# The conditioner's units in pairs, four of the seven products of a unit each split into seven smaller ones

## The chip, the cores and the metric

The kernel runs on one core of a Trainium2 chip, in fp32. The metric is the device time of a whole run, in microseconds (us). The engines are TensorE (PE; matrix products), VectorE (DVE) and GpSimd (POOL; both element-wise), ScalarE (ACT; copies and functions) and SyncE (SP, which here issues DMAs). PE reads weights and tokens from SBUF and writes to PSUM, which has eight banks of 128 partitions x 512 columns.

## The reference

x holds 1024 tokens of 512 features. Two blocks are added to it in turn; the change touches the first stage of the first block, the conditioner.

```python
# the conditioner: 512 -> 1376 -> 512, with an adapter of rank 16 chosen for each batch
gate = lora_add(einsum('bnh,fh->bnf', x, W_gate), x, A_gate, B_gate)
up   = lora_add(einsum('bnh,fh->bnf', x, W_up),   x, A_up,   B_up)
act  = silu(gate) * up
down = lora_add(einsum('bnf,hf->bnh', act, W_down), act, A_down, B_down)
# the first feed-forward layer: 512 -> 1792 -> 512, weights w * (su @ sv) of rank 4
d = silu(linear(down, gate_w, ...)) * linear(down, up_w, ...)
x = x + linear(d, down_w, ...)
# then a second block of the same kind, on the new x: one product with adapters, and int4 weights with scales
```

## The kernel before

**Stages.** Features lie on the partitions, tokens on the columns. The order of the work is: the conditioner's gate and up ("c"), its down projection (down_c), the first feed-forward layer's gate and up ("f") and down, then the second block (layers "l" and "q"). Gate and up are worked through in units of 128 hidden features: 11 units in c (1376 padded to 1408), 14 in f.

**Seven products.** gate_up (L543) computes one unit. It sees the unit's two weight blocks (gate, up) by two halves of the features as a 2x2 matrix, and the tokens likewise as two halves of the features by two halves of the tokens (TB = 512 columns). Instead of eight block products it makes seven, after Strassen and Winograd: products 1 to 7, each of two matmuls of 128x128 weights by 128x512 tokens into one bank (product, L352). Four weight forms (s1 to s4, differences of weight blocks) are made on DVE or POOL by gate_up_forms (L389) and weight_forms (L297), and four token forms T1 to T4 once for all units. DVE adds the banks up into act; ACT takes the silu; POOL multiplies (L606, L611). The adapters come in as eight small matmuls of 32 rows a unit (gate_up_adapters, L966).

**Pairs in layer f.** Units 0 and 1 of f go through gate_up. The others go in six pairs through two_units (L1122). There products 2, 7, 4 and 3 of the two units are split once more: the two units of the pair and two halves of the features give the second level its 2x2 weights, two halves of 256 columns its tokens, so that each of the four becomes seven small matmuls of 128x256 (`small`, L1143), 28 in a pair, and the other three products of each unit stay full. `pair` (L1153) computes two of the four at a time: banks z1 (za1, zb1) and z5 (za5, zb5) take the small products that several outputs share, ACT copies z1 into the result tiles r2, r7 (or r4, r3) and DVE adds z5 at `fifth`. The second-level weight forms are made by POOL in forms_of (L1098), the second-level token forms by DVE once. A pair ends with `finish`, which multiplies the first half of act, and last_silu, which is called in the next pair.

**The order in c.** The loop (from L990) takes units 0 to 10 in turn. prepare_c (L525) loads a unit's weights three units ahead, makes its forms one unit ahead, and at units 8 to 10 loads f's first weights, scales them (scale_f: small products "pw" of scale factors on PE, five a call, then three multiplications on DVE) and makes their first forms. In the same loop stand the splitting and joining of the scale factors (scale_piece: a memset, DMAs by SP, a copy on ACT, a subtraction on POOL, and at the join L474 and L476 on DVE), the gathering of adapter rows for down (POOL, L222) and the loads of the down weights (L383, from unit 3 on, into wd_all).

**What sets the order.** Each engine runs its instructions in the order in which the program lists them (in_order), and waits there for what the others have not yet done. All matmuls but those of layer q go through the helper mm, and carry its line, L88, in the profile. PSUM banks are handed out in turn from a pool of eight: a product's first matmul waits until the last reader of its bank's former content is through.

Of the kernel before, what the change touches and what calls it, by code (L numbers as in the profile page):

```python
# [7 lines left out]
F32 = mybir.dt.float32  # L8
# [5 lines left out]
P = 128  # L14
NB = 8
# [17 lines left out]
AHEAD = 3  # L33
# [22 lines left out]
def kernel(  # L56
# [468 lines left out]
    def prepare_c(f: int):  # L525

        if f + AHEAD < NF0:
            load_c(f + AHEAD)
        if f + AHEAD - 1 < NF0:
            finish_c(f + AHEAD - 1)  # L530
        if f == NF0 - 3:
            load_f(0)
            load_f_down(0)
        if f >= NF0 - 2:
            scale_f(0, f - NF0 + 2)()
        if f == NF0 - 1:
            load_f(1)
            gate_up_forms("f", (0, 1), nc.gpsimd)
# [4 lines left out]
    def gate_up(  # L543
# [69 lines left out]
        for tb in range(NTB):  # L613
            acts[f, tb] = act[tb]
        return finish
# [259 lines left out]
    with ExitStack() as c_layer:  # L875
# [90 lines left out]
        def gate_up_adapters(f: int):  # L966
            def add(banks, fresh, go_on):
                for q2 in range(2):
                    for tb in range(NTB):
                        for s in range(2):  # L970
                            rows = rows4(tb, s)
                            mm(
                                banks[s][tb][:, bass.ts(q2, TG)],
                                b_rows4[rows, q2, bass.ts(f, P)], t0[0][rows, bass.ts(q2, TG)],
                                start=(s, tb) in fresh, stop=(s, tb) in fresh or q2 == 1,
                                skip_group_check=(s, tb) in go_on,
                            )

            return add

        def unit_temp(f: int):
            return lambda what: temps.tile([P, TB], F32, tag=what, name=f"{what}_c{f}", bufs=2)


        first_unit = None
# [6 lines left out]
        for f in range(NF0):  # L992
            prepare_c(f)
            if 2 <= f <= 6:
                join_piece = split_piece()
            if 1 <= f <= 5:
                split_piece = scale_piece(temps, f - 1)
            if f >= 3:
                for of in range(f - 3, f - 2 if f < NF0 - 1 else NF0):
                    load_c_down(of)  # L1000
            if f == 2:
# [3 lines left out]
            if 3 <= f < 7:  # L1005
                down_adapters_a.gather(range(2 * f - 6, 2 * f - 4))
            if f == 8:
                down_adapters_a.arrange(nc.scalar.copy, slice(0, NB))
            finishing = gate_up(
                [act_c[:, f, tb] for tb in range(NTB)], unit_temp(f), "c", f, b_x, gate_up_adapters(f), f == 0, f == NF0 - 1,  # L1010
                (first_low_rank, first_unit) if f == 1 else (),
            )
            if f:
                finishing()
            else:
                first_unit = finishing
            if 2 <= f <= 6:
                join_piece()
# [8 lines left out]
        def down_low_rank():  # L1027
# [5 lines left out]
            )  # L1033

# [17 lines left out]
        with ExitStack() as top:  # L1052
# [4 lines left out]
                {1: down_low_rank, 6: three_forms}, down_adapters,  # L1057
# [6 lines left out]
    with ExitStack() as top:  # L1064
# [5 lines left out]
        def second_tokens(i: int, src: str):  # L1070

            b1, b2 = b_h[src]
            left, right = (bass.ts(q, TB // 2) for q in range(2))
            t = {"3": b1[:, right]}
            for w in ("1", "2", "4"):
                t[w] = temps.tile([P, TB // 2], F32, tag=f"T{w}_{i}", name=f"T{w}_{i}")
            for w, x1, x2 in (
                ("1", b1[:, right], b1[:, left]), ("2", b2[:, right], t["1"]),
                ("4", b2[:, left], t["2"]),
            ):  # L1080
                in_order(nc.vector.tensor_tensor(t[w], x1, x2, ALU.subtract))
            tokens2[i] = {
                1: b1[:, left], 2: b2[:, left], 3: b2[:, right], 4: t["4"],
                5: t["1"], 6: t["2"], 7: t["3"],
            }
# [6 lines left out]
        def scaling(n: int):  # L1092

            return (
                lambda: scale_f(n, 0)(), lambda: scale_f(n, 1)(), lambda: forms_of(n)
            )

        def forms_of(n: int):  # L1098
            a = ready["f", "second", n] = {}
            raw = ready["f", "raw", n]  # L1100

            def second_forms(products, of):
                forms = temps.tile(
                    [P, len(products), 4, P], F32, tag=f"s{products[0]}", name=f"s{products[0]}_{n}"
                ).rearrange("p i w f -> p w i f")
                blocks = [
                    of[:, u].rearrange("p (i c) f -> p c i f", c=2)[:, c]
                    for u in range(2) for c in range(2)
                ]
                weight_forms(nc.gpsimd, *blocks, *(forms[:, w] for w in range(3)), True, s3_to=forms[:, 3])  # L1110
                for j, i in enumerate(products):
                    w11, w12, _, w22 = (w[:, j] for w in blocks)
                    s1, s2, s4, s3 = (forms[:, w, j] for w in range(4))
                    a[i] = {1: w11, 2: w12, 7: s3, 4: w22, 5: s1, 6: s2, 3: s4}

            gate_up_forms(
                "f", (2 * n, 2 * n + 1), nc.gpsimd, True, lambda: second_forms((2, 7), raw[:, :, 2:6])
            )
            second_forms((4,), raw[:, :, 6:8])
            second_forms((3,), ready["f", "s", n][:, :, 4:6])  # L1120

        def two_units(n: int, tail):  # L1122

            fs = (2 * n, 2 * n + 1)
            a, a2 = [ready["f", f] for f in fs], ready["f", "second", n]
            act = [[act_all[:, f, tb] for tb in range(NTB)] for f in fs]
            for f, both in zip(fs, act):
                for tb in range(NTB):  # L1130
                    acts[f, tb] = both[tb]
            two = range(2)

            def temp(what: str, tag: str, bufs: int = 1):
                return temps.tile([P, 2, TB], F32, tag=tag, name=f"{what}_f{n}", bufs=bufs)

            def banks(i):
                return [bank(f"p{i}_f{n}_{u}") for u in two]

            def full(ps, u: int, i: int, src: str):  # L1140
                product(ps, a[u][i], b_h[src], True, True)

            def small(ps, at: int, i: int, j: int, start: bool):  # L1143

                mm(
                    ps[:, bass.ts(at, TB // 2)], a2[i][j], tokens2[i][j], start=start, stop=True,
                    skip_group_check=not start,
                )

            def add(to, x1, x2):  # L1150
                in_order(nc.vector.tensor_tensor(to, x1, x2, ALU.add))

            def pair(z: str, r, order, at):  # L1153

                z1, z5 = (bank(f"z{z}{i}_f{n}") for i in (1, 5))

                def both(ps, j: int, start: bool):  # L1160
                    for m, i in enumerate(order):
                        small(ps, m, i, j, start and m == 0)

                def copied(blocks: slice):
                    size = blocks.stop - blocks.start
                    for m in two:
                        src = z1[:, bass.ts(m, TB // 2)]
                        if size > 1:
                            src = src.unsqueeze(1).to_broadcast([P, size, TB // 2])
                            in_order(nc.scalar.copy(r[m][:, blocks], src))  # L1170
                        else:
                            in_order(nc.scalar.copy(r[m][:, blocks.start], src))

                both(z1, 1, True)
                copied(slice(0, 1))
                both(z5, 5, True)
                at(0)
                both(z1, 6, False)
                copied(slice(1, 2))
                at(1)  # L1180
                both(z1, 7, False)
                copied(slice(2, 4))
                at(2)

                def fifth():
                    for m in two:
                        to = r[m].rearrange("p (i j) t -> p i j t", j=2)[:, :, 1]
                        src = z5[:, bass.ts(m, TB // 2)]
                        add(to, src.unsqueeze(1).to_broadcast([P, 2, TB // 2]), to)

                return fifth

            def r_tile(what: str):
                return temps.tile([P, 4, TB // 2], F32, tag=what, name=f"{what}_f{n}")

            def all_of(r):
# [573 lines left out]
```

## Time and profile before

| | us |
|---|---|
| median of 3 runs (lowest, highest) | 673.28 (672.62, 673.37) |
| the profiled execution | 673.58 |
| its span, first to last instruction | 671.8 |
| c unit 2 | 37.51 to 50.80 |
| c units 3 and 4 | 50.80 to 77.38 |
| c units 9 and 10 | 130.76 to 157.57 |
| down_c | 157.57 to 229.41 |
| one pair of f | 284.02 to 307.67 |

The profile gives for each group of instructions its line, the engine, the operation, the tiles out<-in, shape and count; a timeline gives each stretch of like instructions with its start. "PE p_c" is a conditioner product, "p_f", "za_f", "zb_f" those of layer f, "pw" a scale product. A matmul in fp32 leaves two records. The idle time ahead of a group is given with what ended it.

### The profile page before, as it was taken

The numbers are of one execution on the slowest core, as the hardware profiler recorded it, in microseconds if no ns is written. First come the engines' busy times: TensorE is split into PE (matmuls) and PEld (weight loads), VectorE is DVE, ScalarE is ACT, GpSimd is POOL, SyncE is SP. The second block draws the span as 40 slices with busy tenths as digits, with TensorE's granted clock in tenths as the row PEclk, the third lists the DMA queues.
The fourth block names the chain that finished last, engine by engine and source line by source line (L and its number), as shares of the span: only waits on it lengthen the run. The fifth ranks groups of instructions, "written<-read, shape, count | busy, mean of one in ns | idle before, by whom it ended". The sixth has DMA issues, their size and how long they took to land.

```text
span 671.8 us, 7259 instructions
## 1 busy us (share of the span) xinstructions
PE 661.1 (98%) x2534; PEld 408.3 (61%) x2534; DVE 513.3 (76%) x675; ACT 194.4 (29%) x294; POOL 414.5 (62%) x362
## 2 busy tenths in 40 slices
PE   8999999999999999999999999999999999999995
PEld 3444444444667645666666664785536777788874
DVE  5545544446988996877878689999857888899997
ACT  1122111211111112334323421110115555655563
POOL 5356774432771045668766930898602989898996
PEclk9999999999999999999999999999999999999998
DMA  6501124255002002202200050000931220000003
GB/s 236 201 0 54 64 72 160 93 126 20 1 0 79 32 0 95 94 1 94 95 1 0 1 173 30 1 4 13 344 126 31 55 71 17 17 0 1 0 1 125
DMA packets 39715, 42.48 MB, mean 63 GB/s; under 512 B 24624, under 2 KB 25680, under 8 KB 39552
## 3 DMA queue, kind: packets, MB, share of 16 engines
q1 hardware_dynamic: 33152, 25.71, 12.8%
q0 software_dynamic: 5376, 14.49, 6.9%
q10 hardware_dynamic: 1152, 1.84, 0.8%
q8 instruction: 20, 0.33, 0.2%
q14 instruction: 15, 0.12, 0.1%
HBM read 39.93 MB, written 2.10 MB: 63 GB/s over the span
## 4 chain that ended last, share of the span: by engine, by line
PE 84%; issue 7%; POOL 6%; DVE 1%; DMA 1%; ACT 1%; SPq 0%; POOLq 0%; DVEq 0%; ACTq 0%
PE p_c L88 21%; PE p_f L88 13%; PE gu_q L1485 12%; PE d_f L88 9%; PE d_q L1485 5%; PE d_c L88 5%; PE l L88 4%; PE z_f L88 3%; PE zb_f L88 3%; PE za_f L88 3%; PE z_c L88 2%; POOL sum L1500 1%; PE bank L1485 1%; DMA raw_c<-in_c_gu_dram 1%; POOL act_lo L1500 1%
## 5 line engine op out<-in xcount | busy, mean ns | idle before, releaser
L1494 DVE SCALAR_TENSOR_TENSOR sum<-gu_q,sg,sum 128x1024 f32<-128x1024 f32 x65 | 83.1, 1282 | 15.4 <-ACT sum L1491 10.3
L1485 PE MATMUL gu_q<-h_hi,wgu_q 128*128 128x512 f32 x208 | 82.0, 394 | 0.6 <-DVE l_v L1429 0.4
L1485 PE MATMUL gu_q<-h_lo,wgu_q 128*128 128x512 f32 x208 | 81.1, 390 | 0.0
L88 PE MATMUL p_f<-x,s_f 128*128 128x512 f32 x112 | 52.2, 597 | 0.0
L1500 POOL TENSOR_TENSOR sum<-sum,sum 128x1024 f32<-128x1024 f32 (+1 forms) x14 | 32.6, 2330 | 27.9 <-DVE sum L1494 27.9
L1491 ACT ACTIVATE sum<-gu_q,sg 128x1024 f32<-128x1024 f32 x39 | 43.3, 1112 | 21.6 <-PE gu_q L1485 21.6
L605 DVE TENSOR_TENSOR act_c<-p_c,v_c 128x512 f32<-128x512 f32 x11 | 7.6, 690 | 52.3 <-PE p_c L88 52.3
L1485 PEld LDWEIGHTS gu_q<-h_hi,wgu_q 128*128 128x128 f32 x208 | 39.0, 188 | 12.7 <-DVE x L1494 2.6
L1485 PEld LDWEIGHTS gu_q<-h_lo,wgu_q 128*128 128x128 f32 x208 | 39.1, 188 | 7.9
L88 PE MATMUL p_c<-x,raw_c 128*128 128x512 f32 x88 | 43.1, 610 | 0.5 <-DMA x<-in_xT_dram 0.5
L1500 POOL TENSOR_TENSOR act_lo<-sum,act_hi 128x1024 fp32r<-128x1024 f32 (+1 forms) x15 | 33.9, 2259 | 13.3 <-ACT act_hi L1552 13.3
L1494 DVE SCALAR_TENSOR_TENSOR x<-d_q,sd,x 128x1024 f32<-128x1024 f32 x33 | 42.0, 1274 | 0.0
L88 PE MATMUL p_c<-T_x,raw_c 128*128 128x512 f32 x88 | 41.6, 594 | 0.0
L88 PE MATMUL p_c<-T_x,s_c 128*128 128x512 f32 x88 | 41.2, 592 | 0.0
L88 PE MATMUL p_f<-h,raw_f 128*128 128x512 f32 (+1 forms) x96 | 40.2, 541 | 0.1
L606 POOL TENSOR_TENSOR act_c<-act_c,p_c 128x512 f32<-128x512 f32 x10 | 12.8, 1279 | 41.9 <-DVE act_c L605 33.1
L1500 POOL TENSOR_TENSOR sum<-sum,sil_q 128x1024 f32<-128x1024 f32 (+1 forms) x15 | 33.9, 2261 | 1.6 <-ACT sil_q L1543 1.4
L1485 PE MATMUL d_q<-act_hi,wd_q 128*128 128x512 f32 x88 | 34.8, 396 | 0.0
L1485 PE MATMUL d_q<-act_lo,wd_q 128*128 128x512 f32 x88 | 34.3, 390 | 0.0
L88 PEld LDWEIGHTS p_f<-x,s_f 128*128 128x128 f32 x112 | 20.9, 190 | 19.5 <-issue 16.7
L88 PEld LDWEIGHTS p_c<-T_x,raw_c 128*128 128x128 f32 x88 | 16.6, 190 | 21.4 <-issue 20.5
L88 PEld LDWEIGHTS p_c<-T_x,s_c 128*128 128x128 f32 x88 | 16.7, 190 | 21.0 <-issue 20.3
(349 smaller groups left out, 1519.5 us busy)
## 6 DMA issues: line engine op xcount, KB each, us to landing
raw_f<-in_f_gu_dram SPq DMA_DIRECT2D x14, 512.0 KB
wgu_q<-in_q_gu_dram POOLq DMA_DIRECT2D x14, 512.0 KB
raw_c<-in_c_gu_dram SPq DMA_DIRECT2D x10, 512.0 KB
wd<-in_f_down_dram SPq DMA_DIRECT2D x14, 256.0 KB
wd_q<-in_q_down_dram POOLq DMA_DIRECT2D x14, 256.0 KB
x<-in_xT_dram SPq DMA_DIRECT2D x11, 256.0 KB
wd<-in_c_down_dram SPq DMA_DIRECT2D x11, 256.0 KB
out_dram<-x SPq DMA_DIRECT2D x6, 256.0 KB
```

Of the source, the lines that this page charges most:

```text
L88: in_order(nc_mm(*args, **kwargs))
L605: add(act[0], x4, v, ALU.add)
L606: mul(act[0], act[0], p1, ALU.mult)
L1485: nc.tensor.matmul(ps, w, part[:, at], start=(n == 0), stop=(n == len(src) - 1))
L1491: in_order(nc.scalar.activation(to, ps, AF.Identity, scale=scale))
L1494: nc.vector.scalar_tensor_tensor(to, ps, scale, plus, op0=ALU.mult, op1=ALU.add)
L1500: in_order(nc.gpsimd.tensor_tensor(to, a, b, op))
```

## The change

c's units 2 to 9 are computed in four pairs by the same two_units, which is now a function for both layers. Units 0 and 1 are computed as before, and unit 10 stays single and comes last.

- two_units takes the layer, its tokens and tiles, three callbacks (`amid`), and for c the adapters. With adapters, eight small matmuls for each unit of the pair come at the end of the pair, into two of its product banks and two new ones.
- The second-level tokens (16 subtractions of 256 columns, DVE) are made once, after unit 1, in wd_all's first eight slots, the second-level weight forms in the slots 8 to 11. So the down weights (c's eleven, and f's first two) can't come until the last pair is through: their loads, and those of f's second pair of units, move into unit 10.
- POOL makes all weight forms for a pair in the pair before; those of products 4 and 3 (`rest`, eight operations) at the start of the pair itself.
- Splitting and joining a scale piece happens once in a pair, the last join after unit 10. The gathers for down's adapters come by three, three and two in the first three pairs. Both calls of scale_f for f's first pair come inside unit 10, between its products; their DVE multiplications queue behind the last pair's finishing adds. f's first forms go from unit 10 to a hook inside down_c.
- The result tiles r4 and r3 lie where the up adapters were, r2 in the act of unit 10 or a tile, in turn; p1, u and r7 have one tile each.

```diff
+        tiles = {
+            "r4": up_adapters.raw.rearrange("p b c -> p (b c)"),
+            "r3": up_adapters.a.rearrange("p c b -> p (c b)"),
+        }
+        for what in ("p1", "u", "r7", "r2"):
+            tiles[what] = temps.tile([P, T], F32, tag=what, name=f"{what}_c")
...
+        def second_tokens():
+            for n, (i, src) in enumerate(((2, "21"), (7, "T3"), (4, "T4"), (3, "22"))):
+                places = wd_all[:, 2 * n : 2 * n + 2].rearrange("p i (h t) -> p (i h) t", h=2)
+                tokens2[i] = tokens_of_blocks(b_x[src], *(places[:, j] for j in range(4)))
+
+        def forms_to(products):
+            first = {2: 8, 4: 10, 3: 11}[products[0]]
+            return wd_all[:, first : first + len(products)].rearrange("p i (w f) -> p i w f", f=P)
...
-        for f in range(NF0):
-            prepare_c(f)
-            if 2 <= f <= 6:
-                join_piece = split_piece()
-            if 1 <= f <= 5:
-                split_piece = scale_piece(temps, f - 1)
-            if f >= 3:
-                for of in range(f - 3, f - 2 if f < NF0 - 1 else NF0):
-                    load_c_down(of)
...
+        finishing = unit_c(1, (first_low_rank, first_unit))
+        finishing()
+        second_tokens()
+        rest_of = None
+        for n in range(1, NF0 // 2):
+            for f in (2 * n + 4, 2 * n + 5):
+                if f < NF0:
+                    load_c(f)
+            if n == NF0 // 2 - 1:
+                load_f(0)
+            join_piece = pieces[-1]()
+            if n == 1:
                 a_down_rows, b_down_rows, a1_rows, b1_rows = late_rows()
                 gather_rows(b0_down, b_table, b_down_rows)
                 down_adapters_a = Adapters(l0, temps, "0d", a_table, a_down_rows, NF0)
+            if n < 4:
+                down_adapters_a.gather(range(3 * n - 3, min(3 * n, NB)))
+            else:
                 down_adapters_a.arrange(nc.scalar.copy, slice(0, NB))
+
+            def next_piece():
                 join_piece()
+                pieces.append(scale_piece(temps, n))
+
+            def next_forms():
+                if n + 1 < NF0 // 2:
+                    rest_of_forms.append(forms_of_pair("c", n + 1, forms_to))
+                else:
+                    finish_c(NF0 - 1)
+
+            rest_of = two_units(
+                "c", n, b_x, tokens2, act_c, tiles.get, lambda: spare if n % 2 else tiles["r2"],
+                (lambda r: lambda: r and r(nc.gpsimd.tensor_tensor))(rest_of),
+                (rest_of_forms[-1], next_piece, next_forms), gate_up_adapters,
+            )
+        join_piece = pieces[-1]()
+        load_f_down(0)
+        for f in range(NF0):
+            load_c_down(f)
+        load_f(1)
+
+        def rest_and_scale():
+            silus.append(rest_of(nc.gpsimd.tensor_tensor))
+            scale_f(0, 0)()
+
+        def silus_and_scale():
+            for u in range(2):
+                silus[0](u)
+            scale_f(0, 1)()
+
+        silus = []
+        unit_c(NF0 - 1, (rest_and_scale, silus_and_scale))()
+        join_piece()
...
+        if adapters is None:
...
+        else:
+            for u in two:
+                x1, x8 = (bank(f"p{i}_{layer}{n}_{u}") for i in (9, 8))
+                adapters(fs[u])(
+                    [[x1, b5[u]], [b4[u], x8]], {(0, 0), (1, 1)} | ({(1, 0, 1)} if u else set()),
+                    {(0, 1), (1, 0)},
+                )
+                if u == 0:
+                    fifth43()
+                add(c11[u], x1, c11[u])
+                in_order(nc.scalar.activation(c11[u], c11[u], AF.Silu))
+                add(act[u][0], b4[u], v[u])
+                add(u_[:, u], b5[u], u_[:, u])
+                add(act[u][1], x8, act[u][1])
```

## The prediction

> **What bounds the kernel now.** I read, in this order: busy time by engine, the chain of work that ended last, a table by stage, and the timeline of TensorE (PE) and of the engines beside it. First the busy times and the engines' shares of the chain:
>
> ```profile
> PE 661.1 (98%) x2534; PEld 408.3 (61%) x2534; DVE 513.3 (76%) x675; ACT 194.4 (29%) x294; POOL 414.5 (62%) x362
> PE 84%; issue 7%; POOL 6%; DVE 1%; DMA 1%; ACT 1%; SPq 0%; POOLq 0%; DVEq 0%; ACTq 0%
> ```
>
> PE is busy 98% of the span, so a product less counts, and so does every wait put in front of PE. The stages that matter (columns: stretch, sum, then each engine's busy time with its instructions, granted clock, DMA share, GB/s):
>
> ```profile
> 37.51:50.80 13.29, 13.29 (x49) 5.96 (x45) 6.07 (x14) 2.22 (x4) 6.52 (x7) 1.00 0.00 0
> 50.80:77.38 26.58, 26.58 (x93) 11.92 (x89) 12.10 (x16) 4.74 (x8) 17.39 (x19) 1.00 0.19 60
> 130.76:157.57 26.81, 26.81 (x97) 12.31 (x94) 11.41 (x18) 3.49 (x6) 10.02 (x8) 1.00 0.55 81
> 157.57:229.41 71.84, 71.84 (x337) 47.02 (x333) 66.54 (x86) 11.56 (x24) 30.05 (x28) 1.00 0.12 23
> 284.02:307.67 23.65, 23.65 (x94) 15.63 (x91) 18.85 (x28) 8.30 (x19) 17.89 (x21) 1.00 0.20 68
> ```
>
> The rows are: unit 2 of the conditioner; its units 3 and 4; its units 9 and 10; its down projection; one pair of units of the second layer, which already has the new form. PE has no gap in any, at the full granted clock, while VectorE (DVE) and GpSimd (POOL) have slack in the first three. A pair in the new form has 28 DVE instructions where two units have 16: the slack is what the change spends.
>
> **The products.** The prices come from PE's timeline, start to start:
>
> ```profile
> 52.62 1.88 PE L88 MATMUL p_c<-T_x,s_c 128*128 128x512 f32 x4
> 54.33 1.88 PE L88 MATMUL p_c<-T_x,raw_c 128*128 128x512 f32 x4
> ...
> 284.99 1.03 PE L88 MATMUL za_f<-T,s 128*128 128x256 f32 x4
> 285.85 0.59 PE L88 MATMUL p_f<-h,raw_f 128*128 128x256 f32 x2
> 286.28 1.03 PE L88 MATMUL za_f<-T,s 128*128 128x256 f32 x4
> ```
>
> A full product (two matmuls, four records) takes 54.33 - 52.62 = 1.71 us, 1.716 over a unit; a small one (one matmul 256 wide, two records) 286.28 - 285.85 = 0.43 us, 0.4316 over the pair. A unit's eight adapter matmuls take 1.08 us and 0.1 on each side, since 7 x 1.716 = 12.01 and the unit takes 13.29.
>
> [...] The row decides: 0.4316 is half of one full-width matmul's 0.858 within 1%, in fp32, with weight loads busy for 15.63 of the pair's 23.65 us.
>
> A new pair is then 6 full products (10.30), 28 small (12.08) and two adapter groups (2.36): **24.74 us against 26.58**, -1.84 each, -7.36 for the four pairs (2,3), (4,5), (6,7), (8,9). Unit 10 keeps its form (13.29), but both groups of scale products pw now stand between its products. Where they stood at a unit's end they cost 0.22 each; inside pairs of the second layer, 0.63 (0.43 and 0.1 on each side). So +0.82. PE itself gains **6.55 us**; what follows is given back as waits.
>
> **What DVE and POOL do to one another.** This decides the waits:
>
> ```profile
> 105.89 0.34 DVE L474 TENSOR_SCALAR scale_parts<-scale_parts,keep 128x256 fp32r<-128x256 f32 x1
> 106.27 3.36 DVE L476 SCALAR_TENSOR_TENSOR scale_parts<-scale_raw,keep,scale_parts 128x256 fp32r<-128x256 f32 x1
> ...
> 106.80 1.27 POOL L606 TENSOR_TENSOR act_c<-act_c,p_c 128x512 f32<-128x512 f32 x1
> 108.02 1.27 POOL L611 TENSOR_TENSOR act_c<-act_c,u_c 128x512 f32<-128x512 f32 x1
> ```
>
> A DVE operation with two SBUF inputs, 0.34 us by its width, ended 0.34 us after the second POOL multiplication. DVE adds that read PSUM keep about 0.6 us each beside POOL. [...]
>
> **A: the tokens of the second level, start of the first pair.** Sixteen subtractions of 256 columns (0.34 us, 5.4 in sum) are issued in a block when unit 1's last add is done at 39.44, ahead of the small index operations and of the pair's first add. POOL runs unit 1's multiplications to 41.0 and then the subtraction of a scale piece (1.28). The second product of za5 needs the fifth subtraction. With no collision that is 39.44 + 5 x 0.36 = 41.2; behind the two multiplications and the subtraction 43.5. PE wants it at 42.3. Cost 0 to 1.2, with 2 if the block's tail also holds up the first adds; I take **1.0**.
>
> **B: the rest of the pair's weight forms.** Eight POOL operations of 128 columns stand behind the gathers for b_down and three of ga_0d (1.3 us apart), which wait for DVE's index rows at about 48.0. The gathers end at 52.8, and the first form that zb5's second product needs at 56.6, when PE wants it. Cost 0 to 1.7; **0.3**.
>
> **C: the pair's edges.** At a pair's end DVE's fifth adds free the bank of the next p1 with about 0.1 us to spare. In the next pair ACT has the silus of c12, which wait for a 1024-wide DVE add that ends 6.9 us in (7.7 to 8.9 in the last pair, where POOL's multiplications collide with it), ahead of the copies of za1 that za7 waits for: 0.1 each in the second and third, 0.85 in the last. The joining of a scale piece (1.64 where its width alone needs 0.6) stands ahead of DVE adds that free banks for b5: 0.4. Together **1.6** (0.4 to 4).
>
> **D: unit 10.** pw_0_1_2 takes the bank of pw_0_0_0, which is free when DVE has scaled raw_f with it. On DVE this stands behind the add of product 5 (7.5 us into the unit) and three finishing adds of the last pair, two of 512 and one of 1024 columns. With 0.6, 0.6, 1.22 and 0.6 it ends 10.5 us in; PE wants the bank at 9.45. Cost 1.05. In the second layer's pairs the same kind of adds take 2.29 us for two and 1.47 for the wide one beside POOL: 11.9, cost 2.4. Each waiting as the 3.36 above did: 13.2, cost 3.7. POOL is idle when the first begins, so the low half of these: **1.8**. Behind the waiting PE stand unit 10's last two products and adapters, and all of down.
>
> **Moves that I cost at nothing.** Eleven down weights of the conditioner, two of the second layer, and its second pair of gate and up weights go to unit 10's time, since their places hold scratch. They are 3.4 MB ahead of what is needed first; at the 340 to 420 GB/s that the trace shows in its busiest microseconds that is about 9 us, and they land 7 to 9 us into a unit of over 14.5. SP issues them in 15 x 0.45 = 6.8 us; behind them sd (11.38 us of SP's time) comes some 10 us later and is for a layer far behind. The second layer's first forms (5.1 us of POOL) go into down: POOL is busy there for 30 of 71.84 us, and its forms due next have some 20 us. The last scale piece (1.2 us of DVE) goes ahead of down's first forms; later DVE has an idle 3.3 us there that takes it. The loads of c units come in pairs, 0.45 us each of SP, all ahead of their use by a pair. If the cover of these fails it is the weights that are late, the third rival.
>
> **Sum.** -6.55 + 1.0 + 0.3 + 1.6 + 1.8 = **-1.85 us** on the profiled execution (673.58, span 671.8 and 1.8 around it), so 671.7; it lies 0.3 above the median of the runs, so 671.4 against 673.28. I say **671.5**. With all low ends the costs are 1.5 and the gain 5.0; with all high ones 11.4 and a loss of 4.9.
>
> **Rivals.** [...] *The other side, POOL becomes the bound* (0.30). In the second pair POOL has a subtraction 1.28, three gathers 3.9, the rest 5.35, silu multiplications 2.5, a memset 0.53, the next forms 8.3 and two multiplications 2.5: 24.4 against PE's 24.74; the first has about 23, the third 23.1. In the conditioner's down, with DVE as busy as it will be now, POOL's 256-wide operations take 0.86 to 1.17 instead of 0.73. With 0.2 us more on some 20 operations the pairs need 26.5, 27.5 and 26.5, and PE waits for the rest forms: about 5.3 us in sum. -6.55 + 5.3 + 1.0 + 1.6 + 1.8 = +3.2, **676.5**. It decides from about 24.8 us of POOL work in a pair; against it, the second layer's pairs keep pace with 17.9. *The weights are late* (0.04): at under 170 GB/s, 3.4 MB take 20 us and down starts some 5 us late: **677**. That small products aren't there at all can be left out: each pair's instructions hold 28 of them.
>
> **How the numbers follow.** The likeliest case, the gain mostly given back, has 0.38 (669.7 to 673.3 alone). Within 0.2% (1.35 us), about what a measurement of this kernel can tell from no change, lies a third of it and a little of the others. Faster 0.48, same 0.19, slower 0.33. The range for 8 in 10 takes in the first rival's and most of the second's: 667.8 to 677.0.
>
> **What would show it.** In the profile after: pairs of about 25 to 26 us between starts of p1, PE gaps before za5 in the first pair and before pw_0_1_2 in unit 10, and down with 71.8 us as before. A gap before zb5 with POOL as releaser in each pair would show the second rival; one released by a DMA at down's start the third. Wrong at its root would be a small product over 0.45 us here.

## The result, and the profile after

The changed kernel takes 677.0 us (676.75 to 678.9, 5 runs) against 673.28 (672.62 to 673.37): 1.0066 times as long, 95% interval 1.005 to 1.0083. I had forecast 671.5 and a range up to 677.0 with a gain as the likeliest. The profiled execution took 678.9 us, span 677.1; two of the five runs lie near it and three near 676.8. One stretch of 3.41 us more or less at half the clock (below) would make 1.7 us, about that difference; this is an estimate, since only the one run has a trace.

The page of the kernel after, busy times and chain:

```profile
PE 661.2 (98%) x2630; PEld 429.8 (63%) x2630; DVE 550.6 (81%) x735; ACT 212.2 (31%) x342; POOL 446.1 (66%) x398
PE 76%; DVE 8%; issue 8%; POOL 5%; ACT 1%; DMA 1%; SPq 0%; DVEq 0%; POOLq 0%; ACTq 0%
```

PE's busy time is the same as before, 661.2 us to 661.1, although some 6.5 us of products were taken away; DVE now has 8% of the chain where it had 1%. The stages (stretch, sum, busy time of PE, PE's weight loads, DVE, ACT and POOL, then the granted clock, DMA share, GB/s); the rows are the first, second and last pair, unit 10 up to the end of its scale products, and the rest of unit 10:

```profile
37.51:65.00 27.49, 25.74 (x116) 16.75 (x112) 21.97 (x44) 7.95 (x18) 18.96 (x23) 1.00 0.15 46
65.00:90.33 25.33, 25.27 (x113) 16.83 (x112) 19.47 (x27) 8.68 (x20) 22.02 (x25) 1.00 0.15 53
...
115.61:141.85 26.24, 25.72 (x114) 16.76 (x113) 18.76 (x27) 9.69 (x21) 16.46 (x20) 1.00 0.16 57
141.85:154.49 12.64, 10.52 (x32) 4.41 (x31) 10.52 (x16) 2.71 (x6) 4.83 (x4) 0.97 1.02 317
154.49:162.13 7.64, 7.64 (x25) 3.24 (x24) 2.21 (x4) 0.00 (x0) 4.35 (x5) 0.61 1.61 7
```

No pair reaches 24.74 us, the best take 25.3. In unit 10 the rest, two products and the adapters, takes 7.64 us for what takes 4.7 at full clock (151.55 to 156.26 in the first experiment): the granted clock is 0.61 there. Down starts at 162.13 instead of 157.57, so 4.56 of the 5.3 us that the span has grown are lost by then.

PE's timeline in unit 10:

```profile
149.35 1.98 PE L87 MATMUL p_c<-T_x,raw_c 128*128 128x512 f32 x4
151.26 0.38 PE L87 MATMUL pw<-scale_parts 16*128 16x256 f32 x2
153.77 0.79 PE L87 MATMUL pw<-scale_parts 16*128 16x512 f32 x3 [2.12 <-DVE raw_f L516]
154.49 3.78 PE L87 MATMUL p_c<-x,raw_c 128*128 128x512 f32 x4
158.06 3.07 PE L87 MATMUL p_c<-x,s_c 128*128 128x512 f32 x4
```

The third pw of the second group waits 2.12 us for its bank, and then a full product that takes 1.72 us elsewhere takes 158.06 - 154.49 = 3.57. DVE and POOL ahead of it:

```profile
149.63 1.28 DVE L679 TENSOR_TENSOR act_c<-act_c,ga 128x512 f32<-128x512 f32 x2
150.83 2.29 DVE L679 TENSOR_TENSOR ga<-ga,u_c 128x1024 f32<-128x1024 f32 x1
153.04 1.27 DVE L516 TENSOR_TENSOR raw_f<-raw_f,pw 128x512 f32<-128x512 f32 x2
...
150.39 3.86 POOL L825 TENSOR_TENSOR act_c<-act_c,r_c 128x512 f32<-128x512 f32 x2 [4.84 <-DVE act_c L679]
```

The two narrow adds run unhindered; the wide one takes 2.29 us beside POOL's first multiplication (1.22 without it, in the second experiment), and POOL's two take 3.86 for 2.5. The clock, in steps of one us (columns as above):

```profile
152.00:153.00 1.00, 0.00 (x0) 0.00 (x0) 1.00 (x1) 0.00 (x0) 1.00 (x2) 1.00 1.05 422
153.00:154.00 1.00, 0.23 (x3) 0.24 (x3) 1.00 (x3) 0.79 (x2) 1.00 (x1) 0.81 1.23 154
154.00:155.00 1.00, 1.00 (x4) 0.56 (x5) 1.00 (x3) 0.36 (x1) 1.00 (x2) 0.50 1.54 11
...
160.00:161.00 1.00, 1.00 (x2) 0.11 (x1) 0.00 (x0) 0.00 (x0) 0.00 (x0) 0.78 1.32 5
161.00:162.00 1.00, 1.00 (x17) 0.72 (x16) 0.00 (x0) 0.00 (x0) 0.00 (x0) 1.00 0.77 6
```

It falls to 0.50 at the end of the wait and stays there for 6.8 us (153.61 to 160.44), which costs an estimated 3.4, half of it. And the 25.3 us of an undisturbed pair come from its end; PE and DVE there, in the first pair:

```profile
62.31 2.76 PE L87 MATMUL p_c<-t_gu,b_rows 32*128 32x256 f32 x32
65.00 3.70 PE L87 MATMUL p_c<-x,raw_c 128*128 128x512 f32 x8
...
62.61 1.29 DVE L679 TENSOR_TENSOR ga<-zb_c,ga 128x512 f32<-128x512 f32 x2 [4.41 <-ACT ga L698]
```

The sixteen adapter matmuls take 65.00 - 62.31 = 2.69 us where eight take 1.08 elsewhere. In steps of 0.05 us PE is idle at 63.9, just when DVE's two adds of zb5 end (62.61 + 1.29).

### The profile page after: what moved, and what is told of

The parts are those of the page before. It is cut to its first block, busy times and chain, and to the rows that moved or that the text cites. A ratio compares the mean times of both kernels' runs of the same rounds, so it can differ in the third digit from the quotient of the medians.

```text
span 677.1 us, 7591 instructions
## 1 busy us (share of the span) xinstructions
PE 661.2 (98%) x2630; PEld 429.8 (63%) x2630; DVE 550.6 (81%) x735; ACT 212.2 (31%) x342; POOL 446.1 (66%) x398
## 4 chain that ended last, share of the span: by engine, by line
PE 76%; DVE 8%; issue 8%; POOL 5%; ACT 1%; DMA 1%; SPq 0%; DVEq 0%; POOLq 0%; ACTq 0%
PE p_f L87 13%; PE p_c L87 12%; PE gu_q L1577 12%; PE d_f L87 9%; PE d_q L1577 5%; PE d_c L87 5%; PE l L87 4%; PE z_f L87 3%; PE zb_f L87 3%; PE za_f L87 3%; PE zb_c L87 2%; DVE x L1586 2%; PE z_c L87 2%; DVE sum L1586 2%; DVE ga L679 1%
## 5 line engine op out<-in xcount | busy, mean ns | idle before, releaser
L308 POOL TENSOR_TENSOR wd<-wd 128x256 f32<-128x256 f32 (+1 forms) x6 | 8.5, 1424 | 38.5 <-DVE ds_f L868 23.4
L301 POOL TENSOR_TENSOR s_f<-raw_f 128x512 f32<-128x512 f32 x7 | 10.3, 1476 | 33.0 <-DVE raw_f L516 33.0
L87 PE MATMUL p_c<-x,raw_c 128*128 128x512 f32 (+1 forms) x64 | 31.6, 624 | 0.2 <-DMA x<-in_xT_dram 0.2
L87 PE MATMUL d_c<-act_c,wd 128*128 128x512 f32 (+1 forms) x72 | 28.2, 526 | 0.0
L87 PEld LDWEIGHTS p_f<-h,raw_f 128*128 128x128 f32 x96 | 18.1, 190 | 15.5 <-issue 13.8
```

The lines of the kernel that those rows point to most:

```text
L87: in_order(nc_mm(*args, **kwargs))
L301: in_order(engine.tensor_tensor(s1, a21, a22, ALU.add))
L308: made = engine.tensor_tensor(to, x1, x2, ALU.subtract)
```

## The experiments

Where a kernel has one run, spans are compared; a span lies about 1.8 us under its run's time. The kernel after has a span of 677.1, the one before 671.8. Unit 2, with which the first pair begins, started between 36.81 and 38.36 us in all these traces, ahead of every edit, so a difference of spans of about 1 us says little by itself; smaller effects are read from the lines.

**The scale products' multiplications ahead of the adds.**

```diff
         def rest_and_scale():
-            silus.append(rest_of(nc.gpsimd.tensor_tensor))
             scale_f(0, 0)()
+            silus.append(rest_of(nc.gpsimd.tensor_tensor))
```

> In unit 10 the three multiplications with the first scale products are put ahead of the last pair's finishing adds on DVE; nothing else. Theory: the 2.1 us wait of PE before the third pw product falls away, and with it the stretch of 6.8 us at half the granted clock that follows it (153.8 to 160.6), which costs about 3.2 us: unit 10 takes about 15 us instead of 20.28, the run 671.7. Rival 1: the clock falls because of what else happens in unit 10 (3.4 MB of DMA at a share above 1.0), not because of the wait: the wait goes, the low clock stays, 674.9. Rival 2: the wait only moves to the next product or to down's first form, which now stand behind the delayed adds: 676 to 677.

Measured: 672.72 us (672.38 to 673.36), 0.9993 times the kernel before (0.9984 to 1.0002), span 671.3. PE's timeline:

```profile
151.12 0.50 PE L87 MATMUL pw<-scale_parts 16*128 16x256 f32 x5
151.55 1.98 PE L87 MATMUL p_c<-x,raw_c 128*128 128x512 f32 x4
153.37 1.88 PE L87 MATMUL p_c<-x,s_c 128*128 128x512 f32 x4
...
156.26 8.85 PE L87 MATMUL d_c<-act_c,wd 128*128 128x512 f32 x20
```

The wait is gone and the clock is 1.00, with the DMA as before: unit 10 takes 14.56 us (141.70 to 156.26) instead of 20.28, where I had worked out 14.55 without a wait. Two lines in another order are worth 5.8 us between the profiled spans (4.3 between the medians): about 3.4 for the clock, worked out as half of 6.8, and the other 2.3 for the wait of 2.12 and the restart behind it. The DMA alone doesn't bring the clock down (rival 1): its share is 1.35 from 149.00 to 156.26 here, and 1.32 from 149 to 157 in the kernel after. Nothing moved on (rival 2).

**The wide add first.**

```diff
+                if n == NF0 // 2 - 1:
+                    add(all_of(r3), all_of(r3), u_.rearrange("p u t -> p (u t)"))
                 for u in two:
                     add(act[u][0], act[u][0], c21[:, bass.ts(u, TB)])
             for u in two:
                 in_order(mul(act[u][0], act[u][0], c11[u], ALU.mult))
-            add(all_of(r3), all_of(r3), u_.rearrange("p u t -> p (u t)"))
```

> In the last pair's finish the 1024-wide add goes ahead of the two 512-wide ones, so that POOL's multiplications start only behind it. Theory: the wide add took 2.29 us for 1.22 because it stood behind POOL; without that, PE's wait is about 1.1 us instead of 2.1. The first pair's wait of about 1.1 left the clock at 1.00; if the clock falls by the length of a wait, it stays up here too, and the run takes about 672.8. Rival: the length isn't what counts, any wait in this stage brings the clock down: about 675.9. Second rival: the collision with POOL isn't the cause of the 2.29: wait 2.1 as before, 677.

Measured: 674.19 us, span 672.4, PE's wait before that pw 1.05 us, the product behind it at full pace (154.42 - 152.60 = 1.82 us), the mean granted clock 0.997 as in runs of the kernel before (0.997 to 0.999). The wide add:

```profile
149.10 1.22 DVE L679 TENSOR_TENSOR ga<-ga,u_c 128x1024 f32<-128x1024 f32 x1
```

So the collision with POOL made half of the wait, and a wait of half the length leaves the clock up: the step from 1.05 to 2.12 us of waiting costs 4.7 us of span.

**What brings the clock down: waits put into the kernel before.**

```diff
+                def stall(f=f, dummy=act_c[:, NF0 - 1, 0]):    # between products 5 and 4 of unit f
+                    for _ in range(STALLS[f]):
+                        in_order(nc.vector.memset(dummy, 0.0))
+                    mm(bank(f"stall_{f}"), ready["c", f][4][0], dummy, start=True, stop=True)
```

> The kernel before, with a wait of PE put into units 3 to 8 of the conditioner ahead of product 4: PE there takes one more matmul (0.86 us) that needs a chain of 1, 2, 3, 4, 6 and 8 memsets of 512 columns on DVE, behind DVE's add of product 5. Waits of about 0.7 us plus 0.3 to 0.5 for each memset, so about 1.1 to 3.1, or to 4.9. No DMA to speak of in most of these units. Theory: up to some length of wait, between 1.1 and 2.1 us, the granted clock stays at 1.00 and the unit is longer by the wait and 0.86; above it the clock is 0.50 for 3 to 7 us and the unit longer by another 1.7 to 3.4. Rival: the low clock needs unit 10's DMA, and no unit here shows it.

> The kernel before with one memset ahead of the extra matmul in each of units 3 to 8: six equal gaps of 2.07 us, 16.46 us apart. In the run with growing stalls the clock fell only at the end of stretches of 3.41 us in which PE had done nothing, 20.48 us (six such stretches) apart, and gaps of 2.07, 2.73 and 3.39 that lay across the edge of two such stretches left it at 1.00. In the changed kernel a gap of 2.1 us brought it down for two such stretches. Theory: the clock is judged by the share of idle time in stretches of 3.41 us that run on by themselves; at 0.46 busy it stays, at about 0.35 it falls. The gaps here move by 0.18 of a stretch from one to the next, so two or three of six lie within one stretch (busy share 0.39) and bring the clock down, the others don't. Rival: only a whole idle stretch counts, none falls, and what fell in unit 10 has a further cause, the matmuls of 16 rows beside the gap or the DMA.

> The kernel before with two memsets ahead of the extra matmul in each of units 3 to 8: six gaps of 2.07 us, 16.46 us or 4.82 stretches of 3.41 us apart, so that each lies 0.18 of a stretch further. The run with one memset had gaps of 1.42 only, and none brought the clock down. Theory: the idle share of a stretch decides; two or three of the six gaps lie within one stretch (idle share 0.61) and bring the clock to 0.50 for 3.41 us or twice that, 1.7 or 3.4 us each: span between 693 and 700. Rival: 0.61 isn't enough either, clock 1.00 throughout, span 671.8 + 6 x 2.95 = 689.5; then the gap in unit 10 must have had help from what stood beside it.

Growing waits (span 703.2): the gaps were 1.42, 2.07, 2.73, 3.39, 4.71 and 6.02 us. Up to 3.39 the clock stayed at 1.00; behind 4.71 and 6.02 it was at 0.50 for 3.4 and 6.8 us. It fell at 129.07 and 149.55, 20.48 us or six stretches of 3.41 apart, and both gaps held a whole such stretch. By that a gap of 2.1 us could not have brought it down. Six equal gaps: they came out at 1.42 us, not 2.07 as I wrote in the expectation, because one memset was too few; none brought the clock down (span 687.9), which tells nothing on 2.07. With two memsets (span 695.3):

```profile
76.75 1.10 PE L89 MATMUL stall<-act_c,raw_c 128*128 128x512 f32 x2 [2.08 <-DVE act_c L1015]
93.20 1.56 PE L89 MATMUL stall<-act_c,raw_c 128*128 128x512 f32 x2 [2.07 <-DVE act_c L1015]
111.36 1.10 PE L89 MATMUL stall<-act_c,raw_c 128*128 128x512 f32 x2 [2.08 <-DVE act_c L1015]
127.82 2.04 PE L89 MATMUL stall<-act_c,raw_c 128*128 128x512 f32 x2 [2.08 <-DVE act_c L1015]
145.98 1.10 PE L89 MATMUL stall<-act_c,raw_c 128*128 128x512 f32 x2 [2.07 <-DVE act_c L1015]
```

Two of six equal gaps brought it down, at 93.69 and 127.83, ten stretches of 3.41 us apart: the matmul behind them takes 1.56 and 2.04 us instead of 1.10. Laid over these stretches, the two gaps lie wholly inside one (2.07 of 3.41 us idle, 0.61). The gap before 76.75 has 1.96 us in one stretch (0.57) and left the clock up, like the others, which are cut further in. So these runs fit a clock that is judged stretch by stretch: it fell where PE idled for 0.61 of one and was left at 1.00 where it idled for 0.57. The beat doesn't come with the program: this kernel and the one with growing waits differ only in how many memsets stand in a wait, and counted from the start of the span the clock fell at 127.83 us in the one and at 129.07 in the other, 1.24 us or 0.36 of a stretch apart. The growing waits agree: no stretch that left the clock up was idle for more than 1.89 us (0.55). The matmul behind a gap reads zeros, but that doesn't make it count as idle: the stretch from 108.59 to 112.00 in that run had 1.55 us of idle time and 0.93 of such a matmul, 0.73 together, and the clock stayed.

**Matmuls of few rows beside the wait.** In unit 10, 1.97 us of gap (0.58) lay in the stretch from 150.20 to 153.61, hardly more than what left the clock up here, but pw matmuls of 16 rows stood beside it.

```diff
-                    mm(bank(f"stall_{f}"), ready["c", f][4][0], dummy, start=True, stop=True)
+                    mm(to, w[:16], b_x["11"][0][:16], start=True, stop=True)    # ahead of the gap
+                    mm(to, w[:16], dummy[:16], start=True, stop=True)           # behind it
```

> The same with three memsets and with two matmuls of 16 rows (0.86 us each) in place of the one of 128 rows, one ahead of the gap and one behind, as the scale products stand beside the gap of unit 10: gaps of about 1.87 us between 0.86 us of 16-row work on each side. Theory if 16 rows count as little activity: low activity lasts 3.6 us, over half of a stretch lies in it for any position, and the clock falls in most of the six units. Rival: a matmul counts whatever its rows, the gaps of 1.87 do no more than those of 2.07: clock 1.00, span 671.8 + 6 x 3.6 = 693.

Measured: gaps of 1.59 us, not 1.87, shorter than any above that counted, and the clock fell in all six units, once for 3.4 and five times for 6.8 us (span 713.4, mean granted clock 0.971). In the second of the units:

```profile
76.11 1.12 PE L89 MATMUL stall<-x,raw_c 16*128 16x512 f32 x2
78.82 2.07 PE L89 MATMUL stall<-act_c,raw_c 16*128 16x512 f32 x2 [1.59 <-DVE act_c L1015]
80.81 3.78 PE L89 MATMUL p_c<-T_x,raw_c 128*128 128x512 f32 x4
```

Had only idle time counted, none could have: 1.59 us is 0.47 of a stretch, and 0.57 was too little. So 16-row matmuls count for less than others. How much less can be bounded: the stretch that ended at 78.54 had 1.32 us of idle time and 1.12 of 16-row work, so to pass the 1.96 that left the clock up, over half of that work must count as idle, if one share decides in both runs. The six are not six independent cases: the units came 20.44 to 20.48 us apart, six stretches, so the last five lay almost alike on the beat. By this the scale products beside the wait of unit 10, 0.38 us in its stretch, add to what counts as idle there. Whether its gap of 0.58, between the 0.57 that stayed and the 0.61 that fell, would have done it without them isn't shown.

The traces also tell one stretch from two. The clock stayed low for a second stretch where the first low one again held idle time and 16-row work of 0.94 us or more (0.15 and 0.79 in the kernel after, from 153.61 to 157.03), and came back after one where these were at most 0.17 us. Between the two nothing was measured.

**The tokens in two parts.**

```diff
-        second_tokens()
+        second_tokens(((0, 2, "21"), (1, 7, "T3")))     # the steps of the two products in turn
...
                 a_down_rows, b_down_rows, a1_rows, b1_rows = late_rows()
+                second_tokens(((2, 4, "T4"), (3, 3, "22")))
```

> The second-level tokens of products 2 and 7 are made step by step in turn, so that za5's second product needs the second subtraction, not the fifth; the tokens of products 4 and 3 come after the index rows for the gathers, which so start about 3 us earlier. Theory: the waits of 1.24 us before za5 and 0.78 before zb5 in the first pair fall away, the pair takes 25.4 us instead of 27.49: 675.0. Rival: the eight subtractions left ahead of the first add still hold back the freeing of banks, and at most one of the two waits goes: 676.

Measured: span 675.2 (676.98 us), the first pair 25.27 us (37.78 to 63.05) and both waits gone. -1.9 us of span, as the theory had it; the wait of unit 10 and its low clock were the same as in the kernel after.

**The adapters in another order.**

```diff
+                places = [(q2, tb, s) for q2 in range(2) for tb in range(NTB) for s in range(2)]
+                if (1, 0, 1) in fresh:                   # the second unit of a pair
+                    places.sort(key=lambda place: place[1:] == (1, 1))
```

> On top of the kernel with the scale products' multiplications first (profiled span 671.3, 672.7): in each pair the second unit's two adapter matmuls into the bank of x8 go last of its eight. That bank is the one of zb5, which DVE's two fifth adds free 1.5 us after the first unit's adapters begin. The adapters of a pair took 2.69 us instead of 2 x 1.08. Theory: the missing 0.53 us is PE waiting for that bank; moved back by six matmuls the wait shrinks to about 0.1, so -0.4 in each of four pairs: span 669.7. Rival: sixteen matmuls of 32 rows in a row are simply slower, or the wait is of the whole group: no change, 671.3.

Measured: span 672.4. PE's idle moment disappeared, but the sixteen matmuls took 2.69 us as before, so this run said nothing for the bank. It became plain beside the others: the next product started 1.11 us behind the end of DVE's adds of zb5 here too (64.75 and 65.86), because the last two matmuls, which alone need the bank, now ran one behind the other. The 1.0 us that the span is longer than in the kernel with the scale products first is there when the first pair starts (38.36 against 37.35 us), ahead of the edit.

> The three edits together: scale products' multiplications first, tokens in two parts, second x8 last. Theory: the waits that they take away are apart from one another, so the gains add: 672.7 - 2.0 - 1.6 = 669.1, 0.6% under the kernel before. Rival: with PE earlier, DVE and POOL are late at the next place, and half of the 3.6 comes back: 671.

Measured: 670.85 us (670.57 to 671.1), 0.9964 (0.995 to 0.9977): 1.9 below the first edit alone, all from the tokens. Neither the theory's 669.1 nor the rival's reason.

**The last pair.**

```diff
-            else:
-                down_adapters_a.arrange(nc.scalar.copy, slice(0, NB))
...
             def next_piece():
+                if n == 4:
+                    down_adapters_a.arrange(nc.scalar.copy, slice(0, NB))
```

> The three edits, the wide add ahead of the two narrower ones at every pair's end, and ACT's copy of the gathered rows for down (1.36 us) moved from the start of the last pair to its middle. Theory: the two waits of za in the last pair (that pair took 26.24 us, its neighbour 25.28) come from that copy, which stands ahead of the copies of p1 and za1, and from the wide add behind POOL's multiplications, so -0.9 against the three edits: 668.2. Rival: only one of the two counts, 668.7.

Measured: 669.65 us (669.49 to 670.07), 0.9946 (0.9933 to 0.996). -1.2; no wait of za in the last pair is left. Both causes went in one run; their shares are read from the kernel after, where PE lost 0.34 us before the za behind ACT's copy of the gathered rows, and 0.43 before the one behind the silu that waits for the wide add.

**The adds of zb5 in two steps.**

```diff
             copied(slice(1, 2))
+            if split:                                    # z == "b", with adapters
+                for m in two:
+                    add(r[m][:, 1], z5[:, bass.ts(m, TB // 2)], r[m][:, 1])
             at(1)
...
-                    add(to, src.unsqueeze(1).to_broadcast([P, 2, TB // 2]), to)
+                    add(r[m][:, 3], src, r[m][:, 3])
```

> The kernel with scale first, tokens in two parts, wide add first and ACT's copy moved, without the reordering of the adapters. New: the adds of zb5 at a pair's end are cut in two, those onto the second blocks (two of 256 columns) made earlier, right behind ACT's copies of these blocks, when DVE idles for over 2 us; at the end only two of 256 columns are left (0.7 us in place of 1.2). In every kernel so far, the reordered one too, the next product started 1.10 to 1.12 us behind the end of these adds. Theory: they set when the second unit's adapters get their bank; they end 0.45 us earlier, so each pair is 0.45 shorter: 669.6 - 1.8 = 667.8. Rival: matmuls of 32 rows set the 2.69 us themselves: 669.6 as without it, or more, for four more DVE instructions a pair.

Measured: 668.2 us (668.16 to 668.93), 0.9925 times the kernel before (0.9911 to 0.9938). PE, and DVE beside it, at the first pair's end:

```profile
59.85 2.39 PE L87 MATMUL p_c<-t_gu,b_rows 32*128 32x256 f32 x32
...
60.15 0.91 DVE L679 TENSOR_TENSOR ga<-zb_c,ga 128x256 f32<-128x256 f32 x2 [1.62 <-ACT ga L698]
```

The adds end at 61.06 and the next product starts at 62.17, again 1.11 later; the sixteen matmuls take 2.32 us, so 0.37 of the 0.53 us is gone in each pair. DVE's adds set the end of a pair, and still do, by the 0.16 us that 2.32 is over 2 x 1.08. No other wait of PE shows in the conditioner's pairs; they take 24.9 to 25.1 us.

**More work for POOL.**

```diff
         def rest():
+            if layer == "c" and n in (2, 3):
+                in_order(nc.gpsimd.memset(dummy[:, 1], 0.0))
+                for _ in range(4):
+                    in_order(nc.gpsimd.tensor_tensor(dummy[:, 0], dummy[:, 1], dummy[:, 1], ALU.subtract))
```

> On top of the kernel with the scale products' multiplications first (span 671.3): POOL gets a memset and four subtractions of 512 columns that nothing uses (0.5 + 4 x 1.28 = 5.6 us), ahead of the eight rest forms of the second and third pair. There POOL is busy about 22 of 25.3 us. Theory: what decides isn't the sum but when a form is due: the first rest form that zb5 needs is ready about 3.8 us early in the second pair, so PE waits about 1.8 us in each of the two pairs, and the forms of the next pair, which are 1.4 us early, follow late: 675 in span. Rival (the second one of the prediction): POOL has no room, all 5.6 us come through in both pairs: 682. Other rival: it is hidden altogether, 671.3.

Measured: span 679.0, +7.7, of which 0.4 is there at the start of the first pair. The second pair took 29.47 us and the third 28.36, so of 5.6 us 4.1 and 3.1 came through. What PE waited for (0.6 of the first row belongs to the first pair):

```profile
PE zb_c L87 <- POOL wd L301: 3.5, 4, 1.6
PE zb_c L87 <- ACT ga L705: 3.1, 2, 1.6
```

The forms were late by 2.9 us in the two pairs, where I had worked out 3.6; as much again came by way of ACT, whose copies of zb1 go into the tile that POOL's last multiplications still read. So for work ahead of the rest forms POOL had 1.5 us to spare in the second pair and 2.5 in the third. With its 22.0 and 21.7 us of work, that puts the point from which it holds PE up at an estimated 23.5 to 24.2 us a pair, near the second rival's 24.8. That is for this place in POOL's queue only: with the added work it was still busy for only 27.0 of 29.46 us, so it was the time at which forms were due that counted, as the theory had it, and work put elsewhere wasn't tried.

**Layer q.** The last 0.7 us of the span come up far from the change.

```diff
+                    mm(bank(f"stall_{f}"), ready["c", f][4][0], b_x["11"][0], start=True, stop=True)    # unit 3, one kernel
+                        in_order(nc.vector.memset(dummy, 0.0))                                          # unit 3, the other
```

> The kernel before with one matmul more (128x512, its result not used) in the conditioner's unit 3, 0.86 us of PE. In each changed kernel so far, those made from the kernel before too, PE stands 1.4 us before the first product of layer q with no releaser ("issue"), where the kernel before waits 0.4 us for DVE. Theory: the place of PE's instructions in its program decides it, and one matmul more or less moves it: the 1.4 us show, span 671.8 + 0.9 + 1.0 = 673.7. Rival: it takes a longer delay or more instructions: 0.4 us for DVE as before, span 672.7.

> The kernel before with one memset more of 512 columns on DVE in unit 3, no instruction more on PE. Theory: PE's program is as before, so PE waits 0.4 us for DVE ahead of layer q's first product, span 671.8. Rival: the 1.4 us come with any change of the program or of the times, span 672.8.

Measured: spans 673.4 and 671.6. What PE waited for, in the kernel with one more matmul:

```profile
PE gu_q L1497 <- issue: 1.4, 1, 1.4
```

and in the one with one more memset:

```profile
PE gu_q L1496 <- ACT h_hi L1432: 0.4, 1, 0.4
```

One instruction more on PE, and PE stands 1.44 us with no releaser before layer q's first product, 1.08 more than it waits in the kernel before. Eleven kernels here with other PE instructions than that one show it, the changed one among them. The added matmul also delays PE, by about 0.9 us, and the memset doesn't, so these two runs alone don't part the instruction from the delay; but the same 1.4 us show in kernels with spans from 666.7 to 713.4, which speaks for the instructions. What PE does in that time isn't shown.

## Why the prediction was wrong

**The products** came as worked out: small ones 0.43 us apart, unit 10 without its wait 14.56 against 14.55, and a pair without the other waits 24.90 against 24.74, the 0.16 being what is left of DVE's last adds.

**A** was 1.24 us (1.0 forecast) and **B** 0.78 (0.3), for the reasons given; one edit took both away.

**C** had a wrong place. I saw DVE's last adds of zb5 as freeing a bank for the next p1 with 0.1 us to spare. They free one earlier in the same pair, for x8 of its second unit, and PE waits 0.53 us there in every pair; with 0.96 in the last pair and some 0.3 besides, most of it in the first pair, that makes 3.4, where I had 1.6 (0.4 to 4). The causes in the last pair were the ones forecast, and ACT's copy of gathered rows besides, which I had passed over.

**D** is the step that failed. The wait itself cost 2.3 us where I took 1.8, inside its bounds: the wide add did stand behind a multiplication, while the narrow ones did not. (That the third pw came 153.77 - 141.85 = 11.92 us into the unit, as in the middle one of my three sums, is luck: there it was the narrow adds that were to lose most.) But I ended its account with the wait, and put what a wait does to the clock at nothing, without a reason. The fall of the clock behind it cost another 3.4 us, more than the wait, and no bound of mine held it. No run shows why a wait brings the clock down. The traces show by how much and when: 0.50 for one stretch of 3.41 us (129.07 to 132.48 behind the wait of 4.71 us) or for two, where 2.07 us of one stretch or more were idle, or 1.59 beside 16-row matmuls, and no fall behind the wait of 1.05 us in the second experiment. Nor does any run show the reason for which I took the low half of my three sums, that an idle POOL at the start keeps the adds short: in the kernel after the two narrow ones took 1.28 us, begun while POOL waited, and the wide one 2.29 beside it.

The sum that was to be -6.55 + 4.7 = -1.85 was so -6.55 + 1.24 + 0.78 + 3.36 + 5.73 = +4.56 at the start of down, with C as what is left of the four pairs when A and B are taken off; another 0.7 came behind it, with layer q's standstill, for which I had nothing. The clock is the largest of the misses but not the only one: without its 3.4 us the sum would still be +1.1, since C was 1.8 too small and A, B and D's wait together 1.2. So the forecast gain would have failed to come even at full clock. Down itself took in the moved forms, loads and the last scale piece at no cost, as forecast, and no weight came late.

**The rivals.** The time is about that of the second one, POOL as the bound, and by chance: its mechanism isn't there. POOL worked at most 22 us in a pair, its 256-wide forms took 0.73 us as before and not 0.86 to 1.17, and PE waited 0.6 us for it in all. The first, that the waits hardly show (0.28; 668.5), fell too: A and B cost 2.0 us, C 3.4 and D 5.7.

## What to carry to other kernels

A wait in front of a nearly full TensorE had a second price here: where it emptied 0.61 of a 3.41-us stretch, the clock was at 0.50 for one or two more, and where it emptied 0.57, the clock was left at 1.00. So look in the trace for what such a wait does to the clock, also where 16-row matmuls stand beside it (1.59 us were enough there), and keep instructions that free a bank ahead of long element-wise work in their engine's queue: here two lines in another order were worth 5.8 us between the profiled spans. Pairs were then worth 0.75% over the kernel before, but only with nearly every small wait that they had brought removed, each read off as "next product so many us behind the end of that add".

## What the runs showed that I had not expected

The granted clock fell with 2.07 of 3.41 us idle and not with 1.96, by where the wait lay on a beat that differs from run to run (127.83 us against 129.07). Over half of the time of the 16-row matmuls must count as idle by the 1.32 and 1.12 us of one stretch: beside them 1.59 us were enough, in all six units. With one more instruction on PE a standstill of 1.44 us came some 440 us later.
